# Float8 rounding from the transposes, with an 8-bit quotient in four parts, and another order of the last half blocks

## The chip, the core and the metric

The kernel runs on one core of one Trainium2 chip. The metric is the device time of one run in microseconds (us); lower is better. The engines of a core that matter here are TensorE (PE in the profile: matrix products and transposes), VectorE (DVE), ScalarE (ACT) and GpSimdE (POOL). SyncE (SP) issues the transfers between memory and the chip. Each engine takes its instructions in the order of its own queue; an instruction that waits holds up all that stand behind it on that engine.

## The reference

A decoder of four layers works on 32 sequences of 64 tokens, 2048 tokens of 128 features. Each layer has self attention, cross attention with a context of the same shape, and a feed forward part, each followed by a residual addition and a layer norm without parameters. The change lies in the last layer:

```python
x = _layernorm(x + _L3_attn_ref(x, ...))             # self attention, 16 heads of 8, rotated, causal
x = _layernorm(x + _L3_xattn_ref(x, ctx_1024, ...))  # cross attention, two masks, no output projection
x = _layernorm(x + _L3_ffn_ref(x, ...))
return x

def _L3_ffn_ref(x, kernel, input_scale, kernel_scale, bias):
    x = x.astype(jnp.bfloat16)
    s_in = input_scale[0]
    s_k = kernel_scale[0]
    x_q = (x.astype(jnp.float32) / s_in).astype(jnp.float8_e4m3fn)
    k_q = (kernel.astype(jnp.float32) / s_k).astype(jnp.float8_e4m3fn)
    y = jnp.dot(x_q.astype(jnp.float32), k_q.astype(jnp.float32))
    y = y * (s_in * s_k)
    return y.astype(jnp.bfloat16) + bias
```

The point is the two casts to float8: a quotient is rounded to four significant bits (fewer for small numbers), and it must fall on the side on which the float32 quotient falls.

## The kernel before

**Tiling.** The 2048 tokens are NBLK = 4 blocks of 512 (TB), each of TPB = 4 tiles of 128 tokens. `xt[blk]` holds a block with tokens on the partitions, `xT[blk]` the same with features on the partitions, as the products need it. The parts of the layers are named l0a, l0x, l0f and so on; the last three are l3a (self attention), l3x (cross attention) and the float8 linear layer.

**Order.** `Steps` (L259) is a list written out by hand: `sp.at(step, place, f)` registers work, and all of it is issued sorted by step and then by place (a number such as 5.5), so that the parts of several layers interleave. PE's instructions are issued in just this order. Those of DVE, ACT, POOL and SP start from it, and a scheduler of the framework may still move them on their engine. SBUF tiles come from rotating pools: `q2` has 25 buffers of 512 columns, `q4` 10 of 1024, so a tile also waits for the release of the one that had its buffer before. PSUM has two score buffers of 1024 columns (`S`) and four of 512 (`G`), shared by all else.

**Attention** (`attn8`, L618). A block has four steps, one for each of its pairs of batches and head halves, 16 steps in all from step `base` on. In a step, PE forms the scores (a masking product and 16 small ones, `s`); DVE takes the maximum (`mx`, L598) and subtracts it (`p`, L338); ACT takes the exponential (L601). Two steps later PE transposes the result (`ptps`, place 2), ACT copies it from PSUM (`pT`, L614), and PE multiplies it with the values (`o`, place 5). After every second step DVE divides by the sum (`rec`, `a`). In l3a, `a` is then transposed (`aT`) and multiplied with the output weights. `out` adds the residual (`z`), `normal_x` calls `norm` (L458: statistics on DVE, the root on POOL through `rstd` (L419), the normalized `x` on POOL or DVE). `resid` adds a bias row on POOL. The projections `k`, `q`, `v` of block b are at the steps base + 4b - 4 to base + 4b - 2, place 4. At the end of a block, `turn_x` (L494) transposes `x` on PE (L498) into a PSUM tile and ACT copies that to `xT` (L501). In l3x the last block is split into two halves of two tiles each (`split=True`, `halved`): each half has its norm and its transposes of its own, the first half's at (base + 17, 5.5), the second's at (base + 20, 6).

**Rounding to float8** (`rounding`, L1570) works on the columns of one block, one half block or the weights. From `x` and the scale's parts (`scale_parts`, L1560: 1/s, -1/s, and s split into a high part of 12 bits and a rest) it makes five parts, which are called one after the other: `start` (ACT multiplies by 1/s into a float32 tile `qh`, DVE masks it to 12 bits by `high`, L1556), `remainder` (two scalar_tensor_tensor instructions: `qh` times s, less `x`, exactly), `quotient` (the corrected quotient `qe`, its exponent by a mask, and from that a number `em` whose addition rounds at the wanted bit), `rounded` (add `em`, subtract it), `checked` (two instructions, which turn what overflows float8 into NaN; the result is `xq` in bfloat16). That is one ACT instruction and ten DVE instructions.

**The linear layer** (`fp8_linear`, L1601), called with base = that of l3x + 9. `weights` loads `kin` and `fbias` on SP, forms the scales, and rounds the weights to `kq`; its place is (n - 4, 1.5), where n is l3a's first step. For each block there are eight places: `start` (ACT casts `xT` to bfloat16, `xb`, and prepares the five parts), five times `step` (one part of the rounding at each), `product` (PE multiplies `xq` by `kq` into `y`; ACT scales that to `yb`, DVE adds the bias, POOL, or DVE for half blocks, adds `xt` to give `z`), and `ended` (`last_norm`, L1664: statistics, `rstd`, and the normalization, on ACT for whole blocks and on DVE for half blocks; then the transfer to the output on SP). Blocks 0 to 2 spread these over four steps; the two halves of the last block do all eight in a row, at (base + 9, 3.6) and (base + 11, 7).

Of the kernel before, what the change touches and what calls it, by code (L numbers as in the profile page):

```python
# [20 lines left out]
P = 128  # L21
B, S, D = 32, 64, 128
NT = B * S
NBLK = 4
# [249 lines left out]
class Decoder:  # L274
# [227 lines left out]


# [114 lines left out]
    def attn8(self, sp, base, name, src=None, rope=None, scale=1.0, row=None, mask=(None, None), has_out=True, split=False, number=False):  # L618
# [31 lines left out]
        def turn(n):  # L650
            pTs[n] = self.attn8_turn(prs.pop(n))
# [58 lines left out]

        def normal_x(m):
            blk, i = divmod(m, 2)
            if halved(blk):
                self.norm(blk, zs[blk], None, number, (2 * i, 2))
            elif i == 1:
                self.norm(blk, zs.pop(blk), True, number)

        sp.at(base - 4, 3, start)
        for blk in range(NBLK):
            for i in range(3):  # L720
                sp.at(base + 4 * blk - 4 + i, 4, lambda blk=blk, i=i: prepare(blk, i))
            sp.at(base + 4 * blk + 2, 5.5, lambda blk=blk: resid(blk))
            if halved(blk):
                sp.at(base + 17, 5.5, lambda blk=blk: self.turn_x(blk, (0, 2)))
                sp.at(base + 20, 6, lambda blk=blk: self.turn_x(blk, (2, 2)))
            else:
                sp.at(base + 4 * blk + 8, 6, lambda blk=blk: self.turn_x(blk))
        for n in range(4 * NBLK):
            sp.at(base + n, 0, lambda n=n: score(n))
            sp.at(base + n + 2, 2, lambda n=n: turn(n))  # L730
            sp.at(base + n + 2, 5, lambda n=n: values(n))
# [838 lines left out]
    def rounding(self, dst, x, p, n):  # L1570
# [5 lines left out]
        h, e, m = (self.q2([P, n], name) for name in ("qh", "qe", "em"))  # L1576

        def start():
            nc.scalar.mul(h, x, p[:, 0:1])  # L1579
            self.high(h, h)  # L1580
# [14 lines left out]
        def checked():  # L1595
            nc.vector.tensor_scalar(m, e, 7.3e35, 0.0, ALU.mult, ALU.mult)
            self.tt(dst, e, m, ALU.add)

        return start, remainder, quotient, rounded, checked

    def fp8_linear(self, sp, base, prepared):  # L1601
# [5 lines left out]
        def weights():  # L1607
# [8 lines left out]
            for f in self.rounding(k["q"], kin, self.scale_parts(self.rows["s_k"]), D):  # L1616
                f()

        def start(t0, n):
            blk, t = divmod(t0, TPB)  # L1620
            xb = self.q2([P, TB], "xb", BF16)[:, 0 : n * P]
            nc.scalar.copy(xb, self.xT[blk][:, t * P : (t + n) * P])
            xq[t0] = self.q2([P, TB], "xq", BF16)[:, 0 : n * P]
            parts[t0] = list(self.rounding(xq[t0], xb, k["in"], n * P))
# [27 lines left out]
        for b in range(NBLK - 1):  # L1652
            s = base + 4 * b
            pieces.append((4 * b, 4, [(s, 1.5), (s, 1.6), (s, 5.2), (s + 1, 2.2), (s + 1, 5.2), (s + 2, 2.2), (s + 2, 4.5), (s + 3, 2.2)]))
        s = base + 9
        pieces.append((12, 2, [(s, 3.6 + 0.01 * i) for i in range(8)]))
        pieces.append((14, 2, [(s + 2, 7 + 0.01 * i) for i in range(8)]))
        for t0, n, at in pieces:
            fs = [lambda t0=t0, n=n: start(t0, n)] + [lambda t0=t0: step(t0)] * 5
            fs += [lambda t0=t0, n=n: product(t0, n), lambda t0=t0, n=n: ended(t0, n)]  # L1660
            for place, f in zip(at, fs):
                sp.at(*place, f)

# [20 lines left out]
def decoder_kernel(ctx: ExitStack, tc: tile.TileContext, ins, at, out):  # L1684
# [36 lines left out]
    k.attn8(sp, n + 16, "l3x", c, scale=s8, row=rows["l3x_bv"], mask=("batch", "mask3"), has_out=False, split=True)  # L1721
    k.fp8_linear(sp, n + 16 + 9, (n - 4, 1.5))
# [25 lines left out]
```

## Time and profile before

| what | us |
|---|---|
| runs, in order | 1477.14, 1467.24, 1461.73 |
| median of the runs | 1467.24 |
| the profiled execution's own run | 1467.96 |
| its span, first to last instruction | 1466.2 |
| PE busy in the span | 1228.0 (84%) |
| DVE busy | 929.0 (63%) |
| POOL busy | 737.6 (50%) |
| ACT busy | 694.1 (47%) |
| mean granted clock of TensorE | 0.889 |

One execution is recorded by the profiler. Its span is 1.8 us shorter than the run that it belongs to. Each engine's busy time is the sum over its instructions; the granted clock is the share of its full speed at which TensorE was allowed to run, which is either 1.00 or 0.50 at any moment of this trace, and 0.889 is its mean over the span. Memory is not busy: the page gives 29 GB/s as the mean over the span, and in the last 254 us the DMA engines are busy 4% of the time.

By stretch of the span, with the busy us of each engine:

| stretch, us | PE | DVE | ACT | POOL | clock |
|---|---|---|---|---|---|
| 0 to 230 | 198.02 | 141.28 | 97.57 | 126.97 | 0.92 |
| 230 to 850 | 549.87 | 428.13 | 321.88 | 363.84 | 0.97 |
| 850 to 1212 | 295.48 | 195.36 | 160.61 | 145.43 | 0.81 |
| 1212 to 1466.2 | 184.60 | 164.27 | 114.08 | 101.33 | 0.79 |

The code that the change touches runs in the last row. In the lines of the profile below, L335 is the helper `mm` (a product on PE), and L338 is the helper `tt` (an elementwise instruction on two tensors, on DVE unless POOL is named), so there the tile's name says what is done. An entry like `128x512 f32<-128x512 f32` gives the shape and type of what is written and of what is read; the bracket at the end of a line is the engine's idle time before, and what released it.

### The profile page before, as it was taken

The numbers are of one execution on the slowest core, as the hardware profiler recorded it, in microseconds if no ns is written. First come the engines' busy times: TensorE is split into PE (matmuls) and PEld (weight loads), VectorE is DVE, ScalarE is ACT, GpSimd is POOL, SyncE is SP. The second block draws the span as 40 slices with busy tenths as digits, with TensorE's granted clock in tenths as the row PEclk, the third lists the DMA queues.
The fourth block names the chain that finished last, engine by engine and source line by source line (L and its number), as shares of the span: only waits on it lengthen the run. The fifth ranks groups of instructions, "written<-read, shape, count | busy, mean of one in ns | idle before, by whom it ended". The sixth has DMA issues, their size and how long they took to land. (4 is left out here: it accounts for less than half of the span.)

```text
span 1466.2 us, 36930 instructions
## 1 busy us (share of the span) xinstructions
PE 1228.0 (84%) x16009; PEld 889.8 (61%) x16009; DVE 929.0 (63%) x1831; ACT 694.1 (47%) x1179; POOL 737.6 (50%) x609
## 2 busy tenths in 40 slices
PE   7997888889887898989889995939999853999880
PEld 4775555555555555656667775916677752677670
DVE  5754577777886776666564655635577435676765
ACT  2453444555554554554555542735565312556551
POOL 3534688677785755445542443523355232454531
PEclk9998899999999999999999975969999566999955
DMA  6001010360010000100010002230000001000000
GB/s 231 2 2 24 1 45 1 104 185 2 1 53 1 1 1 2 37 31 2 1 35 32 4 17 60 68 124 2 2 8 5 4 15 32 2 2 3 2 16 14
DMA packets 33714, 43.16 MB, mean 29 GB/s; under 512 B 5946, under 2 KB 27121, under 8 KB 33168
## 3 DMA queue, kind: packets, MB, share of 16 engines
q1 hardware_dynamic: 31536, 38.20, 8.1%
q8 instruction: 126, 2.06, 0.6%
q0 software_dynamic: 2016, 2.60, 0.6%
q14 instruction: 36, 0.29, 0.1%
HBM read 26.63 MB, written 15.56 MB: 29 GB/s over the span
## 5 line engine op out<-in xcount | busy, mean ns | idle before, releaser
L598 DVE TENSOR_REDUCE mx<-s 128x16 f32<-128x1024 f32 x96 | 117.4, 1223 | 127.0 <-PE s L335 125.6
L338 POOL TENSOR_TENSOR turn<-turn,turn 128x1024 f32<-128x1024 f32 x64 | 150.6, 2361 | 92.4 <-DVE turn L338 91.9
L338 DVE TENSOR_TENSOR p<-s,mx 128x1024 f32<-128x1024 f32 (+1 forms) x144 | 158.8, 1103 | 5.0
L614 ACT COPY pT<-ptps 128x512 f32<-128x512 f32 x192 | 104.7, 589 | 92.6 <-PE ptps L612 90.3
L601 ACT ACTIVATE p<-p 128x1024 f32<-128x1024 f32 x96 | 101.6, 1058 | 78.9 <-DVE p L338 77.6
L335 PEld LDWEIGHTS o<-v,pT 128*64 128x64 f32 x3072 | 109.3, 148 | 44.3 <-ACT pT L614 34.6
L549 POOL TENSOR_TENSOR kx<-k,w_const 128x1024 f32<-128x1024 f32 x45 | 85.4, 1917 | 97.8 <-ACT k L542 61.4
L335 PE MATMUL o<-v,pT 128*64 128x18 f32 x3072 | 120.8, 220 | 8.4 <-ACT pT L614 6.2
L335 PE MATMUL s<-kx,q 32*64 32x128 f32 x3072 | 114.6, 286 | 8.0 <-DVE sparts L1558 3.5
L423 POOL TENSOR_SCALAR rstd<-bnmv 128x4 f32<-128x4 f32 (+1 forms) x60 | 16.0, 267 | 198.9 <-DVE bnmv L469 152.5
L612 PE MATMUL ptps<-w_const,p 128*128 128x128 f32 x768 | 115.8, 299 | 0.2 <-ACT c L808 0.2
L335 PEld LDWEIGHTS s<-kx,q 32*64 32x64 f32 x3072 | 89.1, 138 | 44.0 <-issue 40.5
L338 DVE TENSOR_TENSOR turn<-qkps,w_const 128x512 f32<-128x512 f32 (+1 forms) x96 | 75.9, 862 | 53.6 <-PE qkps L335 53.6
L612 PEld LDWEIGHTS ptps<-w_const,p 128*128 128x128 f32 x768 | 96.3, 155 | 9.1 <-issue 8.2
L338 POOL TENSOR_TENSOR rn<-rn,nhalf 128x16 f32<-128x16 f32 x32 | 93.6, 2926 | 2.7
L857 PE MATMUL ropeT<-w_const,turn 128*128 128x128 f32 x512 | 71.1, 285 | 26.2 <-ACT oT L915 12.5
L857 PEld LDWEIGHTS ropeT<-w_const,turn 128*128 128x128 f32 x512 | 58.8, 145 | 39.0 <-ACT oT L915 12.0
L338 DVE TENSOR_TENSOR turn<-qkps,xtab 128x512 f32<-128x512 f32 (+1 forms) x96 | 82.1, 859 | 0.0
L1017 DVE TENSOR_REDUCE rn<-sq 128x16 f32<-128x1024 f32 x32 | 39.0, 1218 | 67.5 <-ACT sq L1013 67.3
L483 POOL TENSOR_SCALAR x<-z,bnmv,rstd 128x128 f32<-128x128 f32 x100 | 79.6, 806 | 2.5
L335 PE MATMUL qkps<-wbig,hT 128*128 128x512 f32 x128 | 72.0, 691 | 10.1 <-POOL hT L993 9.2
L335 PE MATMUL o<-pT,v 64*64 64x64 f32 x2048 | 70.6, 221 | 8.1 <-ACT pT L899 8.1
(331 smaller groups left out, 2731.0 us busy)
## 6 DMA issues: line engine op xcount, KB each, us to landing
sorted_x<-zero SPq DMA_DIRECT2D x9, 990.0 KB, 10.9
wbig<-in_l1f_w_dram SPq DMA_DIRECT2D x4, 1156.0 KB
wbig<-in_l2f_w_dram SPq DMA_DIRECT2D x16, 256.0 KB, 5.3
wbig<-in_l0f_dram SPq DMA_DIRECT2D x2, 1561.0 KB
z<-token_y SPq DMA_DIRECT2D x8, 256.0 KB, 2.9
wbig<-in_l1a_dram SPq DMA_DIRECT2D x1, 1856.0 KB
xsorted<-sorted_x SPq DMA_DIRECT2D x23, 66.0 KB, 1.8
xT<-in_xT_dram SPq DMA_DIRECT2D x4, 256.0 KB, 4.7
```

Source lines behind the costliest of these rows:

```text
L335: self.nc.tensor.matmul(out, lhsT=lhsT, rhs=rhs, start=start, stop=stop)
L338: (eng or self.nc.vector).tensor_tensor(out=out, in0=a, in1=b, op=op)
L423: nc.gpsimd.tensor_scalar(r[:, :n], var, EPS, None, ALU.add)
L483: eng.tensor_scalar(x[:, t0 + t, :], z[:, t0 + t, :], mv[:, t, 0:1], r[:, t : t + 1], ALU.subtract, ALU.mult)
L549: self.wide = eng.tensor_tensor(out=kx, in0=bc(kT, 1, 2), in1=bc(head[:, 2 * i : 2 * i + 2], 2, TB), op=ALU.mult).ins
L598: nc.vector.tensor_reduce(mx, s3, AX.X, ALU.max)
L601: nc.scalar.activation(pr, pr, AF.Exp)
L612: self.nc.tensor.transpose(ps[:, j, :], flat[:, c : c + P], self.ident)
L614: self.nc.scalar.copy(o, ps)
L857: self.nc.tensor.transpose(pt[:, j * P : (j + 1) * P], f[:, j * P : (j + 1) * P], self.ident)
L1017: nc.vector.tensor_reduce(rn, sq, AX.X, ALU.add)
```

## The change

It has four pieces.

1. *The transposes feed the rounding.* `attn8` takes an argument `turned`; with it, the transposes of l3x no longer make `xT`. `turned_low` transposes into PSUM, from where ACT makes both `xb` (bfloat16) and the first quotient `qh`, now also bfloat16, so of eight significant bits. The former three ACT instructions (copy to `xT`, cast to `xb`, multiply into `qh`) become two, and the mask of `qh` on DVE goes. For the weights, ACT makes `kh` in bfloat16 in the same manner.
2. *Four parts.* `rounding` gets `h` as an argument and has no `start`; `checked` is one instruction, a multiplication by 7.3e35 and then by its inverse, which writes `xq` itself. Eight DVE instructions are left of ten.
3. *Places.* `weights` goes from (n - 4, 1.5) to (n + 5, 5.7). In blocks 0 and 1 the four parts keep four of the former places, and the product goes from the base's third step (+2) to its fourth (+3), its norm from +3 to +4. In block 2 all four parts come in a row right after its transposes, in the base's first step, and its product and norm in that step and the next.
4. *The halves.* The first half's rounding goes from 3.6 to 3.1 of its step. The second half's transposes go from (base + 20, 6) to (base + 18, 3.2) of l3x, which is between the first half's rounding (3.1) and its product (3.4) in the same step; then follow the second half's rounding (3.5), its product (3.6), the first half's norm (3.7) and the second's (3.8).

```diff
--- before.py
+++ after.py
@@ -500,6 +500,18 @@
             self.xT[blk] = self.const([P, TB], "xT", bufs=5)
         self.nc.scalar.copy(self.xT[blk][:, t0 * P : (t0 + n) * P], ps[:, 0 : n * P])
+    def turned_low(self, blk, part, s):
+        t0, n = part
+        ps = self.ps8("G", "xTps")[:, 0 : n * P]
+        for t in range(n):
+            self.nc.tensor.transpose(ps[:, t * P : (t + 1) * P], self.xt[blk][:, t0 + t, :], self.ident)
+        xb = self.q2([P, TB], "xb", BF16)[:, 0 : n * P]
+        self.nc.scalar.copy(xb, ps)
+        h = self.q2([P, TB], "qh", BF16)[:, 0 : n * P]
+        self.nc.scalar.mul(h, ps, s)
+        return xb, h
     def attn8_prep(self, blk, w, src, rope, scale, bqs, quick):
@@ -615,7 +627,8 @@
             out.append(o)
         return out
-    def attn8(self, sp, base, name, src=None, rope=None, scale=1.0, row=None, mask=(None, None), has_out=True, split=False, number=False):
+    def attn8(self, sp, base, name, src=None, rope=None, scale=1.0, row=None, mask=(None, None), has_out=True, split=False, number=False, turned=None):
@@ -647,7 +660,7 @@
             blk, pp = divmod(m, 2)
             prs[n] = self.attn8_scores(blk, pp, gg, prep[blk][0], mask)
-        def turn(n):
+        def turn_p(n):
             pTs[n] = self.attn8_turn(prs.pop(n))
         def values(n):
@@ -708,6 +721,12 @@
         def halved(blk):
             return split and blk == NBLK - 1
+        def turn(blk, part):
+            if turned is None:
+                self.turn_x(blk, part)
+            else:
+                turned(blk, part)
         def normal_x(m):
             blk, i = divmod(m, 2)
             if halved(blk):
@@ -721,13 +740,14 @@
                 sp.at(base + 4 * blk - 4 + i, 4, lambda blk=blk, i=i: prepare(blk, i))
             sp.at(base + 4 * blk + 2, 5.5, lambda blk=blk: resid(blk))
             if halved(blk):
-                sp.at(base + 17, 5.5, lambda blk=blk: self.turn_x(blk, (0, 2)))
-                sp.at(base + 20, 6, lambda blk=blk: self.turn_x(blk, (2, 2)))
+                sp.at(base + 17, 5.5, lambda blk=blk: turn(blk, (0, 2)))
+                second = (base + 20, 6) if turned is None else (base + 18, 3.2)
+                sp.at(*second, lambda blk=blk: turn(blk, (2, 2)))
             else:
-                sp.at(base + 4 * blk + 8, 6, lambda blk=blk: self.turn_x(blk))
+                sp.at(base + 4 * blk + 8, 6, lambda blk=blk: turn(blk, (0, TPB)))
         for n in range(4 * NBLK):
             sp.at(base + n, 0, lambda n=n: score(n))
-            sp.at(base + n + 2, 2, lambda n=n: turn(n))
+            sp.at(base + n + 2, 2, lambda n=n: turn_p(n))
             sp.at(base + n + 2, 5, lambda n=n: values(n))
         for m in range(2 * NBLK):
             if has_out:
@@ -1567,17 +1587,13 @@
         self.tt(p[:, 3:4], s, p[:, 2:3], ALU.subtract)
         return p
-    def rounding(self, dst, x, p, n):
-        nc = self.nc
-        h, e, m = (self.q2([P, n], name) for name in ("qh", "qe", "em"))
-        def start():
-            nc.scalar.mul(h, x, p[:, 0:1])
-            self.high(h, h)
+    def rounding(self, dst, x, h, p, n):
+        nc = self.nc
+        e, m = (self.q2([P, n], name) for name in ("qe", "em"))
         def remainder():
             nc.vector.scalar_tensor_tensor(e, h, p[:, 2:3], x, ALU.mult, ALU.subtract)
@@ -1593,10 +1609,9 @@
             self.tt(e, e, m, ALU.subtract)
         def checked():
-            nc.vector.tensor_scalar(m, e, 7.3e35, 0.0, ALU.mult, ALU.mult)
-            self.tt(dst, e, m, ALU.add)
-        return start, remainder, quotient, rounded, checked
+            nc.vector.tensor_scalar(dst, e, 7.3e35, 1.0 / 7.3e35, ALU.mult, ALU.mult)
+        return remainder, quotient, rounded, checked
     def fp8_linear(self, sp, base, prepared):
@@ -1613,15 +1628,18 @@
             self.tt(k["sc"], self.rows["s_in"], self.rows["s_k"], ALU.mult)
             k["in"] = self.scale_parts(self.rows["s_in"])
             k["q"] = self.once([P, D], "kq", BF16)
-            for f in self.rounding(k["q"], kin, self.scale_parts(self.rows["s_k"]), D):
+            by = self.scale_parts(self.rows["s_k"])
+            h = self.q2([P, D], "kh", BF16)
+            nc.scalar.mul(h, kin, by[:, 0:1])
+            for f in self.rounding(k["q"], kin, h, by, D):
                 f()
-        def start(t0, n):
-            blk, t = divmod(t0, TPB)
-            xb = self.q2([P, TB], "xb", BF16)[:, 0 : n * P]
-            nc.scalar.copy(xb, self.xT[blk][:, t * P : (t + n) * P])
+        def start(blk, part):
+            t, n = part
+            t0 = blk * TPB + t
+            xb, h = self.turned_low(blk, part, k["in"][:, 0:1])
             xq[t0] = self.q2([P, TB], "xq", BF16)[:, 0 : n * P]
-            parts[t0] = list(self.rounding(xq[t0], xb, k["in"], n * P))
+            parts[t0] = list(self.rounding(xq[t0], xb, h, k["in"], n * P))
         def step(t0):
             parts[t0].pop(0)()
@@ -1649,17 +1667,20 @@
         sp.at(*prepared, weights)
         pieces = []
-        for b in range(NBLK - 1):
+        for b in range(NBLK - 2):
             s = base + 4 * b
-            pieces.append((4 * b, 4, [(s, 1.5), (s, 1.6), (s, 5.2), (s + 1, 2.2), (s + 1, 5.2), (s + 2, 2.2), (s + 2, 4.5), (s + 3, 2.2)]))
+            pieces.append((4 * b, 4, [(s, 1.6), (s, 5.2), (s + 1, 2.2), (s + 1, 5.2), (s + 3, 4.5), (s + 4, 5.2)]))
+        s = base + 8
+        pieces.append((8, 4, [(s, 1.6 + 0.01 * i) for i in range(4)] + [(s, 5.6), (s + 1, 3.3)]))
         s = base + 9
-        pieces.append((12, 2, [(s, 3.6 + 0.01 * i) for i in range(8)]))
-        pieces.append((14, 2, [(s + 2, 7 + 0.01 * i) for i in range(8)]))
+        pieces.append((12, 2, [(s, 3.1 + 0.01 * i) for i in range(4)] + [(s, 3.4), (s, 3.7)]))
+        pieces.append((14, 2, [(s, 3.5 + 0.01 * i) for i in range(4)] + [(s, 3.6), (s, 3.8)]))
         for t0, n, at in pieces:
-            fs = [lambda t0=t0, n=n: start(t0, n)] + [lambda t0=t0: step(t0)] * 5
+            fs = [lambda t0=t0: step(t0)] * 4
             fs += [lambda t0=t0, n=n: product(t0, n), lambda t0=t0, n=n: ended(t0, n)]
             for place, f in zip(at, fs):
                 sp.at(*place, f)
+        return start
     def last_norm(self, x, z, n, quick):
@@ -1718,8 +1739,10 @@
     back, later = [(n - 4, 3.5), (n, 2), (n + 2, 6), (n + 4, 6)], (n - 1, 2)
     k.capacity_experts(sp, "l2f", ready, (n - 14, 7), tiles, back, later)
     k.attn8(sp, n, "l3a", rope=k.c["r3"], row=rows["l3a_bo"], mask=("all", "causal"))
-    k.attn8(sp, n + 16, "l3x", c, scale=s8, row=rows["l3x_bv"], mask=("batch", "mask3"), has_out=False, split=True)
-    k.fp8_linear(sp, n + 16 + 9, (n - 4, 1.5))
+    turned = k.fp8_linear(sp, n + 16 + 9, (n + 5, 5.7))
+    k.attn8(
+        sp, n + 16, "l3x", c, scale=s8, row=rows["l3x_bv"], mask=("batch", "mask3"), has_out=False, split=True, turned=turned
+    )
     with (
         tc.tile_pool(name="work", bufs=1) as k.work,
```

## The prediction

> **What bounds the kernel now.** I read the profile in this order: the page (busy tenths and granted clock), the windows of the last 213 us, the waits of PE, then the timeline around each wait, and last the order of the instructions on each engine before and after the change, which tells what follows what but has no time in it. The change touches only the last two attentions and what follows, so the first 1212 us stay.
>
> Windows of the end; the columns are us, busy us (and instructions) of PE, PEld, DVE, ACT, POOL, then granted clock, DMA share, GB/s:
>
> ```profile
> 1253.30:1280.00 26.70, 26.33 (x430) 18.91 (x430) 19.55 (x27) 12.73 (x20) 14.84 (x10) 1.00 0.01 2
> 1280.00:1386.40 106.40, 100.71 (x1833) 76.26 (x1831) 78.04 (x129) 64.84 (x99) 56.55 (x56) 1.00 0.01 2
> 1386.40:1427.40 41.00, 37.69 (x392) 29.75 (x392) 23.51 (x60) 19.00 (x32) 16.05 (x20) 0.50 0.05 14
> 1427.40:1466.20 38.80, 3.49 (x44) 2.20 (x44) 20.58 (x65) 6.49 (x15) 5.51 (x9) 0.54 0.05 14
> ```
>
> Three regimes: to 1386 PE is full at clock 1.00; from 1386 to 1427 it is full at half clock; after 1427 it is almost idle and one chain of small DVE, ACT and POOL instructions runs to the end. PE's waits for the rounded tokens `xq`, from the timeline (start us, us, engine, line, operation, in brackets the idle time before):
>
> ```profile
> 1386.45 0.61 PE L335 MATMUL y<-kq,xq 128*128 128x128 bf16 x4 [4.02 <-DVE xq L338]
> 1417.64 0.61 PE L335 MATMUL y<-kq,xq 128*128 128x128 bf16 x4 [2.24 <-DVE xq L338]
> 1438.87 0.40 PE L335 MATMUL y<-kq,xq 128*128 128x128 bf16 x2 [9.33 <-DVE xq L338]
> 1443.70 0.61 PE L335 MATMUL y<-kq,xq 128*128 128x128 bf16 x4 [4.44 <-DVE xq L338]
> 1456.59 0.40 PE L335 MATMUL y<-kq,xq 128*128 128x128 bf16 x2 [11.85 <-DVE xq L338]
> ```
>
> The first two stand in front of attention work that PE could do. The third holds up the transposes of the last half block, which stand behind it on PE although their input was ready at 1434.3: they run at 1444.1, ACT rounds after another 5.5 us of block 2's norm, and the last rounding starts only at 1452.3. And the first wait costs more than itself (windows of PE alone):
>
> ```profile
> 174.67:178.08 3.41, 1.14 (x11) 1.00 0.00 0
> 1232.80:1236.21 3.41, 0.64 (x14) 1.00 0.09 21
> 1382.98:1386.40 3.42, 0.00 (x0) 1.00 0.00 0
> 1386.40:1389.81 3.41, 3.36 (x42) 0.50 0.02 5
> ```
>
> At the end of each of the first three windows the clock falls to 0.50. After 1386 it stays there for 41 us of almost full PE.
>
> **The change part by part**, against the profiled execution: span 1466.2, run 1467.96 (1.8 around the span; 0.7 above the median of the three, 1467.24).
>
> (a) *Weights' rounding moved* from the norm of l3a's block 0 to l3a's fifth step. At 1219 to 1223.7 its ten DVE instructions alternate with the norm's while PE waits 11.9 us. Eight norm instructions took 2.2 us there (1219.03 to 1221.23) and 1.07 us where they stand alone (1244.30 to 1245.37); the pair of `x` and `nb` lose another 0.3. Gain 1.4; part of the following PE work is at half clock until a window ends at 1229.4, so I take **-1.2**. The load of `kin` (32 KB, 0.44 us to issue, 2.5 to land) is moved past three `z` loads on SP, issued at 1234.5 to 1236.0. It is needed by ACT at 1276.6, 40 us later, and nothing stands behind it on SP until the first output at 1397: nothing. `fbias` stays early on SP.
>
> (b) *Where it lands.* Its ACT instruction (0.40) falls in an idle stretch of 2.1 us, and its DVE instructions (2.3 us) in gaps of 1.7 and 0.8 between the maxima. But the order on ACT changes with it: before, `aT`, two `pT` copies, exp, two `v` copies; after, `aT`, exp, one `v` copy, the two `pT` copies, the other `v`. The rows of before:
>
> ```profile
> 1279.91 1.08 ACT L614 COPY pT<-ptps 128x512 f32<-128x512 f32 x2
> 1281.65 1.06 ACT L601 ACTIVATE p<-p 128x1024 f32<-128x1024 f32 x1 [0.67 <-DVE p L338]
> 1282.61 1.25 ACT L564 COPY v<-vps 64x512 f32<-64x512 f32 x2
> 1281.66 1.06 PE L335 MATMUL o<-v,pT 128*64 128x18 f32 x32
> ```
>
> PE's `o` needs `pT`. Exp cannot begin before 1281.65 (plus 0.3 for one `qe` put ahead of its subtraction), ends at 1283.0, half of `v` 1283.5, first `pT` 1284.1: `o` starts 2.4 later than 1281.66. PE is the bound here, so **+2.3**. On POOL `resid` moves behind four `x` (ends near 1289.3, used by DVE at 1291.1): nothing, with 1.8 us of cover.
>
> (c) *Does that stall drop the clock?* I list PE's idle stretches at clock 1.00. All 15 of 2.7 us and more were followed by a fall to 0.50, and so were six of the eight of 2.0 to 2.5 (at 175.1, 2.27 us, for one). The Trainium skill ("TensorE: Matmul & The Clock Gate", Why this matters for your kernels) asks for no idle gap above some 3 us, as one idle window of 3.4 us throttles. By that rule this stall keeps the clock and costs 0; by the rows, a window with a third of PE work is enough. I follow the rows: it falls, more likely than not. The two earlier falls inside an attention (853.9 and 1133.8) lasted 10.2 us each. In l3a a score step takes 5.3 us (1261.85 to 1283.20 is four), at half clock 6.93 (1404.58 to 1411.51) and more with projections: 10.2 us cold lose 2.4 to 4.6. **+3.5**.
>
> (d) *First product (`y` of block 0) one step later on PE.* Per block the rounding loses `high` (0.46), and a mask plus an addition (0.42 + 0.69) become one tensor_scalar, nearest row `em` 0.42, between 0.41 and 0.69: -1.1 us of DVE per 512 columns. A bf16 quotient leaves the scalar_tensor_tensor rows at 0.69 to 0.75, as the nearest row already reads bf16 `xb` (between 0.42 and 0.75; I take no gain). On ACT three passes (0.58 + 0.62 + 0.72) become two from PSUM (nearest rows 0.58 and `yb` 0.69). Walking DVE's new order with these, block 0's `xq` ends near 1383 to 1384 and its product is due near 1387: **-4.0**. The second product comes after one more `o` and `ptps` (3.8 us), and its wait of 2.24 goes: **-2.2**.
>
> (e) *The tail*, counted from the transposes of block 2 (1424.06 before, output issued at 1460.76: 36.7). After: transposes and two ACT passes 2.3; block 2's eight rounding instructions 5.1 with 0.9 of block 1's norm between; `rec`, `a`, `z`, statistics, `yb` 2.5; `rstd` and `x` of the last half 1.2; half 1's rounding 3.5 with 1.9 of block 2's statistics between; product and `yb` behind block 2's four `last` on ACT 1.8; add and `z` 0.7; half 2's rounding 3.5 with 0.9 of half 1's statistics; product and `yb` 1.0; `yb`, `z`, statistics 1.5; POOL 1.0, `last` 0.6. That is 28.4; some 1 us goes as independent DVE instructions overlap by 0.09: 27.5, **-9.2**. Half 2 is now transposed while half 1 is rounded, so its ACT passes and PE are hidden by DVE; DVE is next on the path.
>
> (f) *Clock after 1386.* Without the 4.02 us gap it does not fall at 1386.4. At full clock a step's PE work is 4.2 us, but DVE needs about 5.0 (in four steps: maxima and subtractions 9.8, `rec` and `a` 1.6, both norms' statistics 3.7, rounding 4.9), so up to 1.9 x 4 = 7.7 us are to be had. But ACT's order puts exp and four `last` (1.7) before the `pT` of step 12: PE then idles up to 2.7 us. By (c) that drops the clock about halfway: **-4**.
>
> Sum: -1.2 + 2.3 + 3.5 - 4.0 - 2.2 - 9.2 - 4 = -14.8, a span of 1451.4, a run of 1453.2; against the median **1452**.
>
> **Rivals.** *Slower:* the clock falls at 1284 as in (c) and is not regained. In l3x 41 us at 0.50 did not bring it back. Each cold step costs 6.93 - 5.3 = 1.6; with the 14.3 of the rest to be eaten it decides from 9 cold steps (about 60 us), and all 20 steps to 1386 give +33 - 14 = +19: 1486. Against it: both earlier falls were over after 10 us, and l3a has projections of 512 columns every few steps; for it: at 1147.5 the clock fell again and stayed low for 54 us. 9%.
> *Cold twice:* as the forecast, but the clock falls again at once near 1386: -10.8, 1456. For it, the halves of `v` and POOL make DVE slower there than my walk. 27%.
> *Warm throughout:* neither (c) nor the fall in (f): -14.3 - 7.7 = -22, 1445. 15%.
> *Not what it says:* `xq` is ready no sooner, because the new norms between the last roundings (10 instructions more than I have counted as covered) hold DVE; the tail gives half: 1457. 9%.
>
> **How the numbers follow.** Forecast 40%, its own range 1448 to 1456. A change of 1% is 14.7 us, about what a measurement of this kernel can tell from none (its three runs spread over 15 us): faster means below 1452.6. The forecast lies on that line, so half of it and a little more, all of the warm case, and a tenth of the two middle ones count as faster: 0.40; since unlisted good luck with the windows of the clock is as likely as bad I put it at 0.47. Slower 0.09, within 1% 0.44. Range 1442 to 1461: it leaves out the slow rival and the ends of the others.
>
> **What would show it.** In the new profile: no rounding instructions between 1219 and 1224; a PE wait for `pT` of about 2 us near 1282 and the clock of the next windows (c); no wait above 1 us before the first two `y` (d); clock 1.00 past 1386 (f); from block 2's transposes to the last output's issue 27 to 28 us, and no transposes behind a `y` that waits (e). I am wrong if the last DVE stretch shows idle time above 4 us, or if l3a stays at 0.50 beyond two projections.

## The result, and the profile after

The changed kernel takes 1460.44 us (median of 13 runs, 1458.44 to 1467.57), the kernel before 1471.92 us (median of 13 runs beside them, 1461.73 to 1477.14). The ratio is 0.9937 with a 95% interval of 0.9916 to 0.9959: 9.3 us less by the ratio, which is that of the two means (1461.83 and 1471.02 us). The forecast was 15 us less. So the direction is right and the size is not.

The profiled execution of the changed kernel has a span of 1462.3 us, 3.9 less than the one shown of before. That number alone misleads. The first 1212 us hold the same instructions in both, but their length varies with the clock: PE's last product before the attention l3a (`bvps`) starts at 1212.12 us before, and at 1214.83, 1205.31 and 1208.92 us in three traces of the changed kernel, in which the clock was at 0.50 for 225.3, 208.2 and 215.0 us up to there. So I count everything below from that product. From it to the end of the span it was 254.08 us before, and 247.47 in the profiled execution of the changed kernel: 6.6 us less.

The windows of the end, in the columns of the windows shown of before (us, then busy us of PE, PEld, DVE, ACT, POOL, then granted clock):

```profile
1253.30:1280.00 26.70, 26.33 (x395) 17.79 (x397) 18.98 (x26) 12.67 (x20) 12.99 (x9) 0.95 0.01 2
1280.00:1386.40 106.40, 102.84 (x1746) 77.91 (x1746) 71.08 (x120) 58.41 (x90) 52.50 (x51) 0.94 0.01 2
1386.40:1427.40 41.00, 39.23 (x504) 31.28 (x495) 29.93 (x63) 20.11 (x31) 17.50 (x22) 0.61 0.03 8
1427.40:1462.20 34.80, 8.37 (x74) 6.32 (x72) 21.66 (x71) 8.43 (x19) 7.96 (x12) 0.50 0.08 23
```

Two things are new. The long middle stretch, at clock 1.00 before, now has a mean of 0.94. And between 1386 and 1427 the clock is only 0.61 on average: it falls 9 us later in the span than before, and then stays low. The first is a loss that the change brings with it; the second is a gain that did not arrive.

PE's timeline around the products `y` (start us, us, engine, line, operation, in brackets the idle time before). For two of them there is no bracket, which means no idle time:

```profile
1399.40 0.63 PE L335 MATMUL y<-kq,xq 128*128 128x128 bf16 x4
1425.34 0.63 PE L335 MATMUL y<-kq,xq 128*128 128x128 bf16 x4
1437.19 0.61 PE L335 MATMUL y<-kq,xq 128*128 128x128 bf16 x4 [3.40 <-DVE xq L1612]
1441.61 0.66 PE L508 MATMUL xTps<-w_const,x 128*128 128x128 f32 x2 [3.81 <-DVE x L483]
1446.86 0.40 PE L335 MATMUL y<-kq,xq 128*128 128x128 bf16 x2 [4.58 <-DVE xq L1612]
1452.57 0.40 PE L335 MATMUL y<-kq,xq 128*128 128x128 bf16 x2 [5.31 <-DVE xq L1612]
```

The waits of 4.02 and 2.24 us in front of the first two products are gone. The transposes of the second half (L508, 1441.61) wait for their own input `x`, and no longer for a product in front of them; the wait of 11.85 us before the last product is 5.31.

By stage, between landmarks on PE (us):

| stage | before | after | difference |
|---|---|---|---|
| `bvps` to block 0's transposes in front of l3a | 12.24 | 10.85 | -1.39 |
| from there to l3x's first scores (l3a) | 103.48 | 112.29 | +8.81 |
| l3x's first scores to those of step 12 | 60.98 | 57.22 | -3.76 |
| step 12 to block 2's transposes | 35.24 | 33.02 | -2.22 |
| block 2's transposes to the end of the span | 42.14 | 34.09 | -8.05 |
| sum | 254.08 | 247.47 | -6.61 |

All but one stage gains. The second loses 8.8 us, more than half of what the four others bring. PE's timeline at that place, in the changed kernel:

```profile
1282.57 1.15 PE L335 MATMUL vps<-w_l3a,xT 128*64 128x64 f32 x32
1285.73 1.70 PE L335 MATMUL o<-v,pT 128*64 128x18 f32 x32 [2.01 <-ACT pT L626]
1287.36 1.04 PE L335 MATMUL s<-causal,identb 128*128 128x512 bf16 x2
1288.33 1.98 PE L335 MATMUL s<-kx,q 32*64 32x128 f32 x32
```

and ACT's, the same execution:

```profile
1281.36 0.37 ACT L701 COPY aT<-aT 128x256 f32<-128x256 f32 x1 [1.83 <-PE aT L699]
1283.67 1.06 ACT L613 ACTIVATE p<-p 128x1024 f32<-128x1024 f32 x1 [1.94 <-DVE p L338]
1284.63 0.57 ACT L576 COPY v<-vps 64x512 f32<-64x512 f32 x1
1285.11 1.05 ACT L626 COPY pT<-ptps 128x512 f32<-128x512 f32 x2
```

ACT stands idle for 1.94 us in front of the exponential, although the input of the two `pT` copies is complete at 1282.20 us: they stand behind it in ACT's queue, with one copy of `v` between. Before the change, the copies came first. PE waits 2.01 us for them, and from then on its instructions take nearly twice as long (the scores 1.98 us, where 1.10 is their time at full clock). In every trace here the clock changes only at points that lie whole multiples of 3.41 us apart; I call such a stretch of 3.41 us a window of the clock. PE's windows there (us, busy us of PE, granted clock; the last two columns are DMA share and GB/s):

```profile
1279.73:1283.15 3.42, 3.42 (x66) 1.00 0.00 0
1283.15:1286.56 3.41, 1.34 (x40) 1.00 0.00 0
1286.56:1289.97 3.41, 3.41 (x53) 0.50 0.02 5
1296.80:1300.21 3.41, 3.41 (x26) 0.50 0.02 5
1300.21:1303.63 3.42, 3.42 (x43) 1.00 0.00 0
1388.96:1392.37 3.41, 3.34 (x75) 1.00 0.00 0
1392.37:1395.79 3.42, 2.42 (x44) 1.00 0.02 5
1395.79:1399.20 3.41, 3.41 (x41) 0.50 0.00 0
```

One window with 1.34 us of work, and the clock is at 0.50 for the next four, 13.65 us, though PE is full in them. The last three lines are the second fall, in l3x: a window with 2.42 us of work, that is with 1.0 us of idle time, is followed by 0.50 again, and this time it stays there to the end of the span. Nearly all of that idle time is one wait for `pT`:

```profile
1393.89 1.37 PE L335 MATMUL o<-v,pT 128*64 128x18 f32 x32 [0.92 <-ACT pT L626]
```

### The profile page after: what moved, and what is told of

The parts are those of the page before. It is cut to its first block, busy times and chain, and to the rows that moved or that the text cites. A ratio compares the mean times of both kernels' runs of the same rounds, so it can differ in the third digit from the quotient of the medians.

```text
span 1462.3 us, 36933 instructions
## 1 busy us (share of the span) xinstructions
PE 1237.0 (85%) x16009; PEld 894.3 (61%) x16009; DVE 926.6 (63%) x1819; ACT 689.5 (47%) x1174; POOL 735.3 (50%) x609
## 4 chain that ended last, share of the span: by engine, by line
PE 55%; DVE 16%; POOL 13%; ACT 8%; issue 5%; DMA 2%; another core or an unknown queue 0%; POOLq 0%; SPq 0%; ACTq 0%; DVEq 0%
PE s L335 12%; PE o L335 9%; PE ptps L624 6%; PE qkps L335 5%; DVE turn L338 5%; PE proj L335 5%; POOL turn L338 4%; PE y L335 4%; PE ropeT L877 3%; POOL rstd L338 2%; ACT pT L626 2%; DVE rn L1037 2%; DVE p L338 2%; POOL rn L338 2%; PE vps L335 2%
## 5 line engine op out<-in xcount | busy, mean ns | idle before, releaser
L335 PE MATMUL s<-kx,q 32*64 32x128 f32 x3072 | 117.7, 291 | 8.1 <-DVE sparts L1578 4.3
```

The lines of the kernel that those rows point to most:

```text
L335: self.nc.tensor.matmul(out, lhsT=lhsT, rhs=rhs, start=start, stop=stop)
```

## The experiments

The theory after the result: the parts of the change that shorten waits do what they should; what is missing went to the clock of PE, in l3a by a stall that the new place of the weights' rounding brings, in l3x by small waits that were left. The rivals: the fall in l3a is chance, as the first 1212 us show that the clock varies; or the missing gain lies in the rounding or in the order of the half blocks.

All stretches are from the same landmarks as in the table; "kernel before" in a ratio is the kernel before on the same chip.

### The weights' place alone, in the changed kernel and in the kernel before

`w_early`: the changed kernel with

```diff
-    turned = k.fp8_linear(sp, n + 16 + 9, (n + 5, 5.7))
+    turned = k.fp8_linear(sp, n + 16 + 9, (n - 4, 1.5))
```

> The changed kernel with only the weights' rounding put back at its former place, (n - 4, 1.5). Theory: its new place costs l3a 2.2 us of waiting for pT and 6.1 us of half clock and saves 1.4 in the norm of l3a's block 0. So here: no wait of PE for pT above 1 us near 1282, clock 1.00 from about 1256 to past 1380, the rounding again between the norm's instructions; about 7 us less than the changed kernel, a ratio to the kernel before of 0.989. Rival: the fall in l3a is one of those that vary between executions, and the weights' place hardly matters; then the fall is there again in this trace or the ratio is 0.994 to 0.995.

Measured: ratio 0.9907 (0.9872 to 0.9943). The wait for `pT` and its fall are gone, the stretch of l3a is 107.03 us instead of 112.29, and the first stage is back at 12.13. The clock did fall twice in l3a for one window of 3.4 us each. The windows in front held 3.05 and 3.06 us of work, each with a single wait of 0.3 us; I have no explanation for these two. L3a is still 3.5 us longer than the 103.48 of before; I put that down to them, which no run shows.

`before_w_late`: the kernel before with

```diff
-    k.fp8_linear(sp, n + 16 + 9, (n - 4, 1.5))
+    k.fp8_linear(sp, n + 16 + 9, (n + 5, 5.7))
```

> The kernel before with only the weights' rounding moved to (n + 5, 5.7). Theory: ACT takes exp and half of v before pT here too, PE waits some 2 us for pT near 1282, the clock falls for 10 to 14 us: +8.3 - 1.4 = +7, a ratio of 1.005. Rival (the stall belongs to the other parts of the change, or the fall is chance): -1.4, a ratio of 0.999.

Measured: ratio 1.0054 (1.0031 to 1.0076): this one line makes the kernel before slower. PE's timeline:

```profile
1278.83 1.15 PE L335 MATMUL vps<-w_l3a,xT 128*64 128x64 f32 x32
1282.67 1.96 PE L335 MATMUL o<-v,pT 128*64 128x18 f32 x32 [2.70 <-DVE em L1596]
1284.57 1.04 PE L335 MATMUL s<-causal,identb 128*128 128x512 bf16 x2
```

The bracket names a DVE instruction that ends at the same moment; that the wait is for `pT` is seen from ACT's timeline, in which the exponential and this time both copies of `v` stand in front of it:

```profile
1279.80 1.06 ACT L601 ACTIVATE p<-p 128x1024 f32<-128x1024 f32 x1 [1.81 <-DVE p L338]
1280.76 1.25 ACT L564 COPY v<-vps 64x512 f32<-64x512 f32 x2
1282.04 1.07 ACT L614 COPY pT<-ptps 128x512 f32<-128x512 f32 x2
```

The stall is there without any other part of the change, 2.70 us long, and so is the fall: the clock is 0.50 from 1282.4 to 1299.4. The stretch of l3a is 113.56 us, 10.1 more than before, the first stage 1.4 shorter. The later stages, which this edit leaves alone, repeat those of before: 60.80, 35.23 and 42.70 us. The stall and its cost belong to the weights' place.

### Fill PE's idle time with work that nobody needs

`fill_l3a`: the changed kernel with, in `values`,

```diff
             o, v = os_[m], prep[blk][0]["v"]
+            if name == "l3a" and n == 4:
+                for _ in range(14):
+                    self.mm(o[:, 288:512], self.identb, self.mask3.rearrange("p n k -> p (n k)")[:, 0:224])
```

> The changed kernel with 14 bf16 products of 224 columns put on PE just ahead of the products o that wait for pT in l3a (they write columns of the PSUM tile that nobody reads; some 1.7 us at clock 1.00). Theory: the fall of the clock comes from PE standing idle in that window. So o starts as late as before (2.0 to 2.3 us late), but the clock stays 1.00 through l3a, and the 6.1 us come back: a ratio of 0.9895. Rival: the clock does not fall for idleness of PE, or the 14 products do not count as work: the fall stays, and the ratio is 0.994.

Measured: ratio 0.9892 (0.9857 to 0.9926). PE's timeline:

```profile
1270.61 1.15 PE L335 MATMUL vps<-w_l3a,xT 128*64 128x64 f32 x32
1272.32 1.50 PE L335 MATMUL o<-mask,identb 128*128 128x224 bf16 x14 [0.56 <-DVE z L338]
1273.77 1.36 PE L335 MATMUL o<-v,pT 128*64 128x18 f32 x32
1275.60 0.67 PE L335 MATMUL s<-kx,q 32*64 32x128 f32 x16
```

From `vps` to `o` it is 3.16 us, to the hundredth what it is in the changed kernel (1282.57 to 1285.73): the stall is untouched, and 1.50 us of it are filled with useless products. The window around it now has 2.79 us of work, the clock stays 1.00, and 16 score products take 0.67 us. L3a takes 106.43 us instead of 112.29. So the fall after the stall costs 5.9 us, and the stall itself only 2.2.

### Another place for the weights' rounding

`w_m3_5`: the changed kernel with `(n - 3, 5)` instead of `(n + 5, 5.7)` in the call of `fp8_linear`.

> The changed kernel with the weights' rounding at (n - 3, 5), where by the order it comes after the rotation of q of block 0, in DVE's wait for the z transfers of block 2, and ACT's order in l3a is that of the kernel before. Theory: the head gain of 1.4 stays, and the 8.3 us in l3a go: a ratio of 0.988, at most 0.6 us of delay of block 2's norm. Rival: the new place delays block 2's norm by the whole 2.3 us of the rounding, which PE waits for: 0.989 to 0.990; or the fall in l3a comes anyway: 0.994.

Measured: 1446.68 us, ratio 0.9857 (0.9823 to 0.9892), below the changed kernel's 0.9937, with intervals that do not touch. PE's timeline at the place of the former stall:

```profile
1285.34 1.15 PE L335 MATMUL vps<-w_l3a,xT 128*64 128x64 f32 x32
1286.33 1.06 PE L335 MATMUL o<-v,pT 128*64 128x18 f32 x32
```

No bracket, no wait. The first stage keeps its gain (10.93 us), and l3a takes 101.85. My 0.6 us of delay were too few: block 2's sum `z` runs 27.4 us after `bvps`, where it is 24.3 in the changed kernel, as three rounding instructions are put in front of the maximum and five behind it. But PE's transposes of the next block are only 0.8 us later (32.1 against 31.2 after `bvps`). The following experiments stand on this kernel, since l3a is undisturbed in it.

### The clock in l3x

`fill_l3x`: `w_m3_5` with the products of `fill_l3a` in l3x's steps 8 to 13:

```diff
             o, v = os_[m], prep[blk][0]["v"]
+            if name == "l3x" and 8 <= n <= 13:
+                for _ in range(12 if n == 12 else 6):
+                    self.mm(o[:, 288:512], self.identb, self.mask3.rearrange("p n k -> p (n k)")[:, 0:224])
```

> The changed kernel with the weights' rounding at (n - 3, 5), and 6 bf16 products of 224 columns (12 in step 12) on PE ahead of the products o of l3x's steps 8 to 13, into columns of the PSUM tile that nobody reads: 0.7 us of work per step at clock 1.00, where PE waits 0.9 to 2.6 us for pT. Theory: the term of the forecast that failed in l3x is the clock. Waits of 0.9 us are enough for a fall, and with PE kept busy it stays 1.00 from about 1256 to block 2's transposes, where the last four steps then take what DVE needs, 5.0 to 5.3 us each: from the scores of step 12 to block 2's transposes 25 us or less (33.0 in the changed kernel's trace, 27.5 in the trace with the weights at (n - 3, 5)), a ratio of 0.982 to 0.984. Rival: the products hold PE up, or the clock falls all the same: 28 us or more, a ratio of 0.986 to 0.989.

Measured: ratio 0.9842 (0.9805 to 0.9878). The window from step 12 to block 2's transposes, first of the changed kernel:

```profile
1395.20:1428.20 33.00, 32.30 (x350) 25.82 (x348) 21.93 (x50) 14.82 (x23) 14.88 (x20) 0.51 0.03 9
```

then of `w_m3_5`:

```profile
1389.70:1417.15 27.45, 24.17 (x353) 19.52 (x349) 22.21 (x50) 14.40 (x23) 14.70 (x20) 0.76 0.04 11
```

then of `fill_l3x`:

```profile
1388.40:1411.90 23.50, 20.98 (x381) 17.21 (x379) 21.23 (x48) 14.08 (x23) 12.83 (x17) 1.00 0.04 13
```

DVE's busy time, the third of the five, is 21 to 22 us in all three. At clock 0.51 PE is full for 33.0 us and sets the time; at 1.00 it has 31 instructions more and 11 us less to do, and the stretch is 23.5 us, close to what DVE needs. Between lies whatever the clock allows. But the end gives a part of it back: from block 2's transposes on it is 35.53 us here and 34.05 in `w_m3_5`, as block 2's product waits 4.86 us for DVE's `xq` instead of 3.40. Of the 4 us that this stretch gains, 2.5 are left at the end of the span. That is about what the ratio has, 0.0015 below that of `w_m3_5`, or 2.2 us; but this is well inside the intervals, so the runs do not tell the two kernels apart.

`after_again1` and `after_again2` are the changed kernel itself, traced twice more.

> The changed kernel once more, for a second trace of the same program. Theory: the wait for pT in l3a and the fall after it belong to the program, so they are there in every trace (2.0 us, then 10 to 17 us at 0.50), while the fall in l3x hangs on 0.9 us of waiting and on where the clock's windows lie: from the scores of step 12 to block 2's transposes anything from 27.4 to 33.0 us. Rival: the fall in l3a is absent here, and was chance in the first trace.

> The changed kernel a third time. As for the second trace: by the theory a wait of 2.0 us for pT and a fall in l3a again, and a stretch of 27.4 to 33.0 us from step 12 of l3x to block 2's transposes; by the rival no fall in l3a.

Measured: 1454.49 and 1452.28 us. PE waits 2.01 us for `pT` in both, the clock is at 0.50 for 13.6 to 13.7 us after it in both, and l3a takes 112.24 and 111.68 us. From step 12 to block 2's transposes it is 32.92 and 27.87 us. So the fall in l3a belongs to the program, and the time lost by that in l3x varies by 5 us. From `bvps` to the end they take 247.29 and 241.58 us; with the first trace, that is 6.6, 6.8 and 12.5 us less than the one trace of before, 8.6 on average, which agrees with the 9.3 of the ratio. (Both executions ran on another chip, on which the kernel before has a median of 1467.41 us, and are faster than all 13 of the result; three traces are a small sample.)

The third trace shows where those 5 us hang. The wait of 0.92 us before step 12 is in all three, in a window with 2.42 us of work each time. In the first two the clock falls after it; in the third it does not, and falls only at 1402.42 us, halfway through the stretch, after a longer wait behind ACT's exponential and its four `last`. PE's timeline, then ACT's:

```profile
1387.24 1.37 PE L335 MATMUL o<-v,pT 128*64 128x18 f32 x32 [0.92 <-ACT pT L626]
1402.97 1.96 PE L335 MATMUL o<-v,pT 128*64 128x18 f32 x32 [2.63 <-ACT pT L626]
1400.81 1.63 ACT L1701 ACTIVATE last<-z,nb,rstd 128x128 f32<-128x128 f32 x4
1402.35 1.04 ACT L626 COPY pT<-ptps 128x512 f32<-128x512 f32 x2
```

`fill_both`: the changed kernel, nothing moved, with both fills.

> The changed kernel, nothing moved, with the fill products of both earlier experiments: 14 in l3a ahead of the o that waits, 6 (12 in step 12) in l3x's steps 8 to 13. Theory: the two falls of the clock are where most of the forecast gain went. From block 0's transposes in l3a to l3x's first scores 106.4 us (112.3 in the changed kernel's trace), from step 12 to block 2's transposes 23.5 to 25 (33.0), the rest as it was; a ratio of 0.982 to 0.986. Rival: the second fill gives nothing beyond the first, as DVE holds the last steps: 0.989.

Measured: l3a 106.54 us, from step 12 to block 2's transposes 25.11 (clock 0.93), from `bvps` to the end 233.77, 13.7 less than the changed kernel's first trace. The stretches are what the theory said, the second a tenth over. The ratio is not: 0.9891 (0.9873 to 0.9909), the same as with the first fill alone, the number of the rival. Of the 13.7 us, 11.0 are there in the trace of `fill_l3a` too (236.52 us from `bvps` to the end), so the traces give the second fill 2.7 us, or 0.002 of the ratio, which is less than the intervals can tell. And the profiled execution is the fastest of the seven (1440.47 us; the others go up to 1454.39). What the second fill does in the executions without a trace stays open.

### The parts that shorten the end

`prod_old`: `w_m3_5` with the products and norms of blocks 0 and 1 a step earlier again:

```diff
-            pieces.append((4 * b, 4, [(s, 1.6), (s, 5.2), (s + 1, 2.2), (s + 1, 5.2), (s + 3, 4.5), (s + 4, 5.2)]))
+            pieces.append((4 * b, 4, [(s, 1.6), (s, 5.2), (s + 1, 2.2), (s + 1, 5.2), (s + 2, 4.5), (s + 3, 2.2)]))
```

> The changed kernel with the weights' rounding at (n - 3, 5), and the products and norms of blocks 0 and 1 a step earlier again, as before the change. Theory: the shorter rounding took away only part of the waits of 4.02 and 2.24, as xq is written 1.3 us after PE could take the first product; so a first wait for xq of 1 to 2 us comes back, and another before the second, about +2.5 us against the same without this edit, a ratio of 0.9875. Rival: the shorter rounding took both waits away by itself and the later place gave nothing: no wait above 0.5, a ratio of 0.9857.

Measured: ratio 0.9914 (0.9881 to 0.9946). PE's timeline:

```profile
1386.94 0.40 PE L335 MATMUL y<-kq,xq 128*128 128x128 bf16 x4 [1.20 <-DVE xq L1612]
1387.27 1.11 PE L335 MATMUL o<-v,pT 128*64 128x18 f32 x32
1388.32 0.60 PE L335 MATMUL s<-mask,identb 128*128 128x512 bf16 x2
1388.85 1.96 PE L335 MATMUL s<-kx,q 32*64 32x128 f32 x32
```

Of the wait of 4.02 us, 1.20 comes back: the shorter rounding took the rest. The second product does not wait. Yet the kernel is slower by 0.0057 in the ratio, over 8 us: the scores after it take 1.96 us, for the clock falls after that wait and stays low for 37.6 us, and the stretch from step 12 on takes 34.54 us instead of 27.43. I expected 2.5 us, for I had counted the wait and not the clock behind it. That the wait keeps the clock low is not shown: the first two traces of the changed kernel have no such wait, and take 33.02 and 32.92 us. PE also waits 1.37 us there for a `pT` that stands behind the earlier norm's `last` on ACT (1.65 us).

`halves_old`: `w_m3_5` with the half blocks in their former order:

```diff
-                second = (base + 20, 6) if turned is None else (base + 18, 3.2)
+                second = (base + 20, 6)
...
-        pieces.append((12, 2, [(s, 3.1 + 0.01 * i) for i in range(4)] + [(s, 3.4), (s, 3.7)]))
-        pieces.append((14, 2, [(s, 3.5 + 0.01 * i) for i in range(4)] + [(s, 3.6), (s, 3.8)]))
+        pieces.append((12, 2, [(s, 3.6 + 0.01 * i) for i in range(6)]))
+        pieces.append((14, 2, [(s + 2, 7 + 0.01 * i) for i in range(6)]))
```

> The changed kernel with the weights' rounding at (n - 3, 5), and the last two half blocks in their former order: second transposes at (base + 20, 6), each half's rounding, product and norm in a row. Theory: of the 8.05 us that the end from block 2's transposes became shorter, some 5 came of this order and 3 of the shorter rounding: that stretch some 5 us longer than in the changed kernel's 34.1 to the end of the span, the second half's transposes again behind a product that waits, a ratio of 0.989. Rival: the shorter rounding and the fewer ACT passes gave nearly all of it: 1 us or less, a ratio of 0.986.

Measured: ratio 0.9904 (0.987 to 0.9939). PE's timeline of the end:

```profile
1424.41 0.61 PE L335 MATMUL y<-kq,xq 128*128 128x128 bf16 x4 [4.25 <-DVE xq L1612]
1435.09 0.39 PE L335 MATMUL y<-kq,xq 128*128 128x128 bf16 x2 [10.07 <-DVE xq L1612]
1435.28 0.63 PE L508 MATMUL xTps<-w_const,x 128*128 128x128 f32 x2
1442.72 0.39 PE L335 MATMUL y<-kq,xq 128*128 128x128 bf16 x2 [6.81 <-DVE xq L1612]
```

The transposes stand behind the product that waits 10.07 us, as before the change. The end takes 36.99 us instead of 34.05: in the traces the order is worth 2.9 us, not 5.

`ten_dve`: `w_m3_5` with the former arithmetic: float32 `qh` and `kh`, and

```diff
         e, m = (self.q2([P, n], name) for name in ("qe", "em"))
+        self.high(h, h)
...
-            nc.vector.tensor_scalar(dst, e, 7.3e35, 1.0 / 7.3e35, ALU.mult, ALU.mult)
+            nc.vector.tensor_scalar(m, e, 7.3e35, 0.0, ALU.mult, ALU.mult)
+            self.tt(dst, e, m, ALU.add)
```

> The changed kernel with the weights' rounding at (n - 3, 5), and the former arithmetic: a float32 quotient masked to 12 bits, and the two instructions at the end, so ten DVE instructions per block instead of eight, in the changed order. Theory: by the sum 1.1 us per block and 0.6 per half, on the path in block 2 and both halves: the end from block 2's transposes 2.3 us longer, and block 0's xq 1.1 later, with 0.5 to 1 us more before its product: +3, a ratio of 0.9875. Rival: the two instructions run in DVE's gaps, the order alone carries the gain: +0.5 or less, 0.986.

Measured: ratio 0.9874 (0.9835 to 0.9913). The end takes 36.51 us, 2.5 more, where the sum had 2.3. The waits before its last three products, by PE's timeline:

```profile
1430.47 0.61 PE L335 MATMUL y<-kq,xq 128*128 128x128 bf16 x4 [5.43 <-DVE xq L338]
1440.55 0.39 PE L335 MATMUL y<-kq,xq 128*128 128x128 bf16 x2 [4.01 <-DVE xq L338]
1447.10 0.39 PE L335 MATMUL y<-kq,xq 128*128 128x128 bf16 x2 [6.15 <-DVE xq L338]
```

Block 0's product, though, comes without a wait here too (the stretch to step 12 is 56.97 us): its later place covers the longer rounding. That part of the expectation was wrong. The ratios of `halves_old` and `ten_dve` have intervals that overlap with that of `w_m3_5`, so the 2.9 and the 2.5 us rest on one trace each.

## Why the prediction was right about the way and wrong about the size

| step | predicted | measured | where |
|---|---|---|---|
| (a) weights out of the norm | -1.2 | -0.8 | -1.39 at the transposes, -0.82 left when PE comes to the stall |
| (b) ACT's order, `o` later | +2.3 | +2.2 | `o` 4.07 later in the span (1281.66 to 1285.73), less 2.71 of a later start, plus 0.82 of (a) |
| (c) the clock falls in l3a | +3.5 | +5.9 | 112.29 less the 106.43 of `fill_l3a` |
| (d) the waits before two `y` | -4.0, -2.2 | -3.8, -2.2 | stages three and four |
| (e) the end | -9.2 | -8.05 | last stage |
| (f) clock 1.00 for half of the last steps | -4 | 0, 0 and -5 | three traces |

**Right: (a), (b), (d), (e).** Each is within 1.2 us. ACT's order, the length of the stall and both waits came as the queues' order and the rows of before had said. From block 2's transposes to the issue of the last output it is 28.7 us, where 27.5 were forecast; the walk's own sum, before 1 us was taken off for overlap, was 28.4. The 8.05 us of (e) come apart as 2.9 for the order of the half blocks (`halves_old`) and 2.5 for the two DVE instructions and the float32 quotient (`ten_dve`); the other 2.6 are left by subtraction, and no run shows whether the fewer ACT passes made them or block 2's four parts, which now come in a row.

**Wrong: the two terms of the clock, the size of (c) and the moment of the fall in (f).** In (c) the mechanism was right: the Trainium skill ("TensorE: Matmul & The Clock Gate", section "Why this matters for your kernels") asks for no idle gap above some 3 us and would have put the term at 0; a stall of 2.01 us dropped the clock in all three traces. But I took 10.2 us of half clock from two earlier falls and lost 3.5 of them; it was 13.65 us, and PE is so full there that 5.9 were lost, 43% of the time at half clock. In (f) the prediction let the clock fall "about halfway" through the last four steps. In the first trace it fell at 1395.79 us, with the first of them (its scores start at 1395.19). What I had overlooked was small: the wait of 0.92 us for `pT` just before step 12, shorter than any in my list of idle stretches. The wait that I had counted on, behind ACT's exponential and four `last`, exists: in the third trace it is 2.63 us long and the clock falls after it, 13.9 us into the 27.9, as forecast. That the first two traces fell earlier and the third did not, after the same wait of 0.92 us, no run here explains; so the forecast of (f) came true in one trace of three, and in that one for its reason. With the clock held, the stretch would have given 9.5 us (33.0 to 23.5, in `fill_l3x`), of which the end took 1.5 back: 8.0, close to the 7.7 I had allowed.

In the first trace (c) and (f) together missed by 6.4 us, and the sum by 8.2 (-14.8 against -6.6). With the third trace's -5, the sum comes to -12.5. The ratio lies between. Of the rivals named, "cold twice" (1456 us) describes the first two traces; the slower one, a fall in l3a that is not regained, did not come: the clock was back after four windows in all three.

**A version better than both.** `w_m3_5` takes the whole change and keeps the weights' rounding out of l3a: 0.9857 against 0.9937. That is 21 us less than before, 6 more than the forecast; the forecast's sum without its (b) and (c) is -20.6, though the agreement is in part luck, as (f) varies. `fill_l3x` has 0.9842, not told apart from it.

## What to carry to other kernels

When a scheduler decides an engine's order, moving some ten instructions that have time to spare can reorder others that have none: compare the whole order on every engine, and look for what is now behind a waiting instruction. Where PE is the bound, price a stall as the stall and the half clock that follows it, here 2.2 and 5.9 us; then another place, or work for nobody in the gap, is worth more than the stall itself. And compare traces from a landmark just before the change: the first 1212 us of the same program differed by 9.5 us between three traces, more than the change brought.

## What the runs showed of the hardware

- A wait of PE well below one window of 3.41 us is enough for the clock to fall: 2.01 us in three traces of three, 0.92 us in two of the same three. Counted over the windows of 3.41 us at clock 1.00 in the first traces of both kernels, from 30 us to 1455 us, by PE's busy time in the window: below 1.5 us, 39 of 39 were followed by 0.50; from 1.5 to 2.5 us, 12 of 52; from 2.5 us on, 6 of 561. So busy time decides most cases, but not all: the wait of 0.92 us lay in a window with 2.42 us of work in all three.
- A full PE does not bring the clock back at once. Of the windows at 0.50 with at least 3.2 us of work in those two traces, 40 of 86 were followed by 0.50 again, and in the changed kernel's first trace the clock stayed low from 1395.79 us to the end. The kind of work goes with it: of these 86 windows, 28 of the 31 that hold some of the narrow attention products `o` (18 columns) were followed by 0.50, and 12 of the 55 without them. No run tests whether these products are the cause, and why the other windows differ stays open.
- Products that nobody reads count as work: 14 bf16 products of 224 columns, 1.50 us, held the clock at 1.00 through a stall of unchanged length.
